# Two transformer layers on one core: blocks 1 and 2 by groups of four chunks, softmax attention of a sequence between the next one's groups, key projection folded into the query

## The chip, the cores and the metric

The program runs on one core of a Trainium2 chip. The metric is the device time of one execution in microseconds (us); smaller is better. Everything is computed in fp32 except one helper tile in bf16. The engines are PE (TensorE, matrix products, which write to PSUM banks), DVE (VectorE), ACT (ScalarE, activation functions), POOL (GpSimd) and SP, which issues the transfers. Each engine works through a queue of its own in order; semaphores make one wait for another.

## What is computed

The input is 8 sequences of 1024 rows of 256 numbers. Four blocks follow one another, each with a layer norm in front and an addition behind. Cut to what matters:

```python
# block 1: decoder layer with linear "flow" attention, 16 heads of 16, causal sums
q, k = sigmoid(heads(Wq, bq)), sigmoid(heads(Wk, bk)); v = heads(Wv, bv)
sink_in  = normal / einsum(q + EPS, cumsum(k) + EPS)          # normal = 1, 2, 3, ...
src_out  = normal / einsum(k + EPS, cumsum(q) + EPS)
cons_sink = einsum(q + EPS, cumsum(k * src_out) + EPS) / normal
cons_src  = clip(einsum(k + EPS, cumsum(q * sink_in) + EPS) / normal, -1, 1)
src_comp = exp(cons_src) / cumsum(exp(cons_src)) * normal
x = (q * sink_in / normal) @ cumsum(k^T (v * src_comp)) * sigmoid(cons_sink)
h = layernorm(inputs + x @ Wo + bo); out1 = layernorm(h + gelu(h @ W1 + b1) @ W2 + b2)
# block 2: feed-forward
relu(x @ w1 + b1) @ w2 + b2
# block 3: attention over the whole sequence, one head of 256
Q, K, V = split(t @ W_qkv.T + b_qkv); softmax(Q @ K.T / 16) @ V
# block 4: gated layer, inputs and weights rounded to FP4 by blocks of 16
fp4_linear(silu(fp4_linear(x, w_gate)) * fp4_linear(x, w_up), w_down)
```

The sums of block 1 run along the sequence, so a chunk of rows needs the sums over the chunks before it. Softmax attention needs the keys and values of all 1024 rows before its first row can be done.

## The kernel before

Rows are handled in chunks of 128 (the partitions), 8 chunks a sequence; four chunks are a group (`G`), two groups a sequence (`NG`). The weights stay in on-chip memory for the whole run. Sequences follow one another in a plain Python loop (L381), unrolled into one long program; a sequence goes stage by stage over all its 8 chunks:

- **Projection** (L386 to L415): layer norm, transposes on PE, one product for query and key (L397), one for the value (L401), additions on DVE, sigmoid on ACT. POOL prepares the residual `res`. The next sequence's input is then requested (L418).
- **Head sums** (L437 to L453), twice over the chunks: `head_sums` adds up a chunk's causal sums by a product with a triangular matrix (L354) and one with a matrix of ones for the chunks before (L356), whose sum POOL carries along in `summed` (L365); DVE does L429, L431 and L432 and the weighting L449.
- **Normalisers** (L456 to L490) by group: exponentials, their running sums, scaling of `v4`.
- **Attention of block 1** (L496 to L618) in four steps a chunk: `score` (transposes, products by head pairs L511, causal mask L519), `attend` (32 small records L544, the sums over earlier chunks L533 and L560), `project` (output product L586 and layer norm), `turn` (transpose into `hT`). `staggered` (L368) runs the steps of several chunks shifted against one another, the last step first, and after each step calls `fill`, which advances the first feed-forward (FFN1) of a group already complete.
- **FFN** (`ffn`, L195): eight hidden tiles of 128 x 512, each two matmuls and an activation; then, chunk by chunk, eight matmuls (L217) and the chunk's `finish`. FFN1 uses Gelu and closes block 1; block 2 (FFN2, Relu) follows for both groups (L623 to L643) after a layer norm of four chunks each.
- **Query, key, value** (L649 to L680) for the two groups: eight products of 512 columns for query and key (L653), and the values.
- **Softmax attention and block 4** (L688 to L784), again four staggered steps a chunk: `attention` (two score banks L695, maximum L702, Exp L710), `values` (transposes of the probabilities, L731, layer norm, FP4 rounding), `gate` (two halves of 352 columns, four banks, L752, Silu L759, product L760, FP4 rounding of 704 columns), `down` (transposes L769, product L773, output).

The FP4 rounding of the weights is a generator, `fp4_weights`, of 14 pieces, called from inside `ffn` after every second hidden tile of the first sequence (L212).

On-chip buffers come from pools with a fixed count: `t256` 8, `t512` 15, `t704` 5, `r256` 11, `r512` 10, `r1024` 7, six PSUM banks for products (`mm_bank`) and two for transposes. A tile can be written only when an earlier user of its buffer is done. The framework that builds the program orders each engine's queue itself from the instructions' dependencies and their place in the program, so a queue may differ from the order of the Python code.

Of the kernel before, what the change touches and what calls it, by code (L numbers as in the profile page):

```python
# [31 lines left out]
def block_stack_kernel(ctx: ExitStack, tc: tile.TileContext, a: dict, out: bass.AP):  # L32
# [8 lines left out]

    nc = tc.nc
# [17 lines left out]
    def t256(name):  # L60
        t = wk.tile([P, D], F32, tag="t256", name=name, bufs=8)
        return t

    def t512(name):
        t = wk.tile([P, 512], F32, tag="t512", name=name, bufs=15)
        return t

    def r256(name):
        t = big.tile([P, D], F32, tag="r256", name=name, bufs=11)
        return t  # L70

    def r512(name):
        t = big.tile([P, 512], F32, tag="r512", name=name, bufs=10)
        return t

    def r1024(name):
        t = big.tile([P, G, D], F32, tag="r1024", name=name, bufs=7)
        return t
# [43 lines left out]
    def load_x(s):  # L122
        tiles = []
        for g in range(NG):
            xg = r1024("xg")
            nc.sync.dma_start(
                out=xg,
                in_=x_dram[s, g * GT : (g + 1) * GT, :].rearrange("(c p) d -> p c d", p=P),
            )
            tiles.append(xg)  # L130
        return tiles

    x_next = load_x(0)
# [23 lines left out]
    wsm = load_tiles("L1_attn_W_qkv", 3 * D, 2)  # L157
    bsm = load_cols("L1_attn_b_qk", 4)
    bsv = load_row("L1_attn_b_v", D)
    wgT = const.tile([P, 2, INTER], F32, name="wgT")  # L160
# [33 lines left out]

    def ffn(inT, wa, ba, func, wb, finish):  # L195

        hidden = []
        for f in range(NF):
            bank = mm_bank()
            for k in range(2):  # L200
                nc.tensor.matmul(  # L201
                    bank,
                    lhsT=wa[:, k, f * P : (f + 1) * P],
                    rhs=inT[:, k, :],
                    start=k == 0,
                    stop=k == 1,
                )
            hf = t512("hidden")
            nc.scalar.activation(hf, bank, func, bias=ba[:, f : f + 1])
            hidden.append(hf)  # L210
            if f % 2:
                next(weight_pieces, None)  # L212
            yield
        for c in range(G):
            bank = mm_bank()
            for f in range(NF):
                nc.tensor.matmul(  # L217
                    bank[:, :D],
                    lhsT=hidden[f][:, c * P : (c + 1) * P],
                    rhs=wb[:, f, :],  # L220
                    start=f == 0,
                    stop=f == NF - 1,
                )
            finish(c, bank[:, :D])
            yield
# [7 lines left out]
    def fp4_exact(src, dst, rows, width, temp):  # L233
# [7 lines left out]
        amax = small([P, INTER // QB], "q_amax", 2)[:rows, :nb]  # L241
# [4 lines left out]
        s = small([P, INTER // QB], "q_s", 2)[:rows, :nb]  # L246
        r = small([P, INTER // QB], "q_r", 2)[:rows, :nb]
# [64 lines left out]
    def t704(name):  # L312
        t = wk.tile([P, INTER], F32, tag="t704", name=name, bufs=5)
        return t

    def fp4_weights():

        for name, dstT in (("L1_ffn_w_gate", wgT), ("L1_ffn_w_up", wuT)):
            for r0, rows in INTER_TILES:
                raw = t704("w_raw")  # L320
                nc.sync.dma_start(out=raw[:rows, :D], in_=a[name][r0 : r0 + rows, :])
                quant = t704("w_quant")
                fp4_exact(raw, quant, rows, D, t704)
                bank = pt.tile([P, 4, P], F32, tag="tr", name="tr")
                for k in range(2):
                    nc.tensor.transpose(
                        bank[:, k, :rows], quant[:rows, k * P : (k + 1) * P], ident[:rows, :rows]
                    )
                nc.scalar.copy(dstT[:, :, r0 : r0 + rows], bank[:, 0:2, :rows])
                yield  # L330
        for n in range(2):
            raw = t704("w_raw")
            nc.sync.dma_start(out=raw, in_=a["L1_ffn_w_down"][n * P : (n + 1) * P, :])
            quant = t704("w_quant")
            fp4_exact(raw, quant, P, INTER, t704)
            for k, (f0, rows) in enumerate(INTER_TILES):
                bank = pt.tile([P, 4, P], F32, tag="tr", name="tr")
                nc.tensor.transpose(bank[:rows, 0, :], quant[:, f0 : f0 + rows], ident)
                nc.scalar.copy(wdT[:rows, k, n * P : (n + 1) * P], bank[:rows, 0, :])
            yield  # L340
# [27 lines left out]
    def staggered(stages, n, between=None):  # L368


        for step in range(n + len(stages) - 1):
            for k in range(len(stages) - 1, -1, -1):
                if 0 <= step - k < n:
                    stages[k](step - k)
                    if between is not None:
                        between()
# [4 lines left out]
    for s in range(B):  # L381
        xs = x_next


        qk, v4, res = [], [], []
        for c in range(NCH):  # L386
            g, i = divmod(c, G)
            n0 = t256("n0")
            layernorm(n0, xs[g][:, i, :])
            n0T = t256("n0T").rearrange("p (k t) -> p k t", k=2)  # L390
            transposed(n0T, halves(n0), nc.scalar.copy)
            rc = r256("res0")
# [15 lines left out]
            qkc = r512("qk")  # L408
# [3 lines left out]
            if i == 0:  # L412
                vg = r1024("v4")
                v4.append(vg)
            nc.vector.tensor_tensor(v4[g][:, i, :], vbank[:, :D], bqkv[:, 2 * D :], ALU.add)  # L415

        if s + 1 < B:
            x_next = load_x(s + 1)  # L418


        groups = range(NG)
        s1 = [small([P, G, 2 * H], "s1", 2) for _ in groups]
        s2 = [small([P, G, 2 * H], "s2", 2) for _ in groups]
        r1 = [small([P, G, 2 * H], "r1", 2) for _ in groups]

        def head_sums(dst, c, cur, before):

            qke = t512("qke")
            nc.vector.tensor_scalar(qke, qk[c], ATT_EPS, None, ALU.add)  # L429
            bank = cumulated(cur, before)  # L430
            nc.vector.scalar_tensor_tensor(qke, bank, ATT_EPS, qke, ALU.add, ALU.mult)  # L431
            nc.vector.tensor_reduce(dst, heads(qke), AX.X, ALU.add)  # L432

        def over_heads(v, g, n):
            return v[:, g * G : (g + 1) * G].unsqueeze(2).to_broadcast([P, G, n])

        carry = None  # L437
        for c in range(NCH):
            head_sums(s1[c // G][:, c % G, :], c, qk[c], carry)
            carry = summed(carry, qk[c]) if c + 1 < NCH else None  # L440
        carry = None
        for g in groups:
            nc.vector.reciprocal(r1[g], s1[g])
            flow = small([P, G, 2 * H], "flow", 2)
            nc.vector.tensor_tensor(flow, r1[g], over_heads(pos, g, 2 * H), ALU.mult)
            for i in range(G):
                c = g * G + i
                w = t512("w")
                nc.vector.tensor_tensor(  # L449
                    heads(w), heads(qk[c]), per_head(flow[:, i, :], 2 * H), ALU.mult  # L450
                )
                head_sums(s2[g][:, i, :], c, w, carry)
# [374 lines left out]
```

## Time and profile before

| | |
|---|---|
| median of 3 runs | 4282.09 us (4281.36 to 4286.14) |
| profiled execution, its own time | 4281.81 us |
| its span, first to last instruction | 4280.1 us |
| mean granted TensorE clock | 0.868 |
| table loads on ACT (L710, L759, L410, L461, L209, one more) | 56 + 56 + 8 + 8 + 8 + 1, 1283 ns each |
| second sequence | 571 to 1101 us |
| first softmax attention's Exp | 371.5 us |

In the page, busy time is given by engine with its share of the span and its number of instructions. A chain of waits is followed back from the last instruction: what released it, or what ran before it on its engine. The granted clock is the share of full speed at which TensorE was let run. A busy TensorE is not TensorE at its best: matmuls are pipelined and their recorded ends are modelled, so the distance from start to start says more than the length of one.

### The profile page before, as it was taken

The page shows a single profiled execution, that of the slowest core. Times are in us where ns is not written, and L with a number is a line of the kernel's source. Part 1 is how long each engine was busy: PE and PEld are TensorE (multiplying, and loading weights), DVE is VectorE, ACT ScalarE, POOL GpSimd, SP SyncE. Part 2 cuts the span into 40 slices and gives each one's busy share as a digit, 9 for nine tenths or more (in the row PEclk, how much of TensorE's full clock was granted, in tenths as well). Part 3 has the DMA queues.
Part 4 walks back from the last instruction along what each step waited for, and adds up shares of the span by engine and source line. Part 5 has one row for each costly group of instructions (what it writes and reads, how often), then busy time and mean ns, then how long its engine had stood idle before and what let it go on. Part 6 is the DMA issues. An engine that isn't in the chain of part 4 may idle for free.

```text
span 4280.1 us, 38297 instructions
## 1 busy us (share of the span) xinstructions
PE 3559.5 (83%) x14180; PEld 2416.9 (56%) x14180; DVE 2096.5 (49%) x4817; ACT 926.7 (22%) x1774; POOL 717.3 (17%) x1297
## 2 busy tenths in 40 slices
PE   7878879888798877988779888898778987789877
PEld 5645557455574555755556555565556655566554
DVE  7675464245642456424564245642456324573244
ACT  1122311223112231122311123111221112211132
POOL 4220031200311003210031200312003120031100
PEclk8889897898888988899888988889888898888988
DMA  3000000000000000000000000000000000000000
GB/s 93 5 11 5 7 13 1 0 2 7 13 1 0 3 5 13 1 0 3 7 12 1 0 3 7 12 1 0 3 7 12 1 1 4 5 2 1 0 4 7
DMA packets 25738, 28.88 MB, mean 7 GB/s; under 512 B 2256, under 2 KB 24528, under 8 KB 25552
## 3 DMA queue, kind: packets, MB, share of 16 engines
q1 hardware_dynamic: 25552, 26.43, 2.0%
q8 instruction: 113, 1.85, 0.2%
q14 instruction: 73, 0.60, 0.0%
HBM read 18.03 MB, written 8.39 MB: 6 GB/s over the span
## 4 chain that ended last, share of the span: by engine, by line
PE 61%; DVE 25%; ACT 6%; POOL 4%; issue 4%; DMA 0%; ACTq 0%; DVEq 0%; POOLq 0%
PE mm L201 12%; PE mm L217 8%; PE mm L773 8%; PE mm L752 8%; PE mm L544 6%; PE tr L189 4%; PE mm L397 3%; PE mm L653 2%; PE mm L511 2%; POOL ln_rstd L173 2%; DVE x_amax L295 2%; DVE n L178 2%; DVE ln_st L167 2%; DVE qke L431 1%; DVE s L432 1%
## 5 line engine op out<-in xcount | busy, mean ns | idle before, releaser
L171 POOL TENSOR_SCALAR ln_ve<-ln_mv 128x1 f32<-128x1 f32 x384 | 107.7, 280 | 2718.7 <-DVE ln_mv L169 2703.0
L773 PE MATMUL mm<-wdT,hqT 128*128 128x256 f32 (+1 forms) x768 | 351.6, 615 | 174.7 <-ACT hqT L190 174.7
L773 PEld LDWEIGHTS mm<-wdT,hqT 128*128 128x128 f32 (+1 forms) x768 | 219.1, 313 | 279.7 <-ACT hqT L190 192.6
L544 PEld LDWEIGHTS mm<-v,sc 128*128 128x128 f32 x2048 | 279.2, 218 | 8.8 <-DVE sc L519 8.8
L544 PE MATMUL mm<-v,sc 128*128 128x16 f32 x2048 | 277.6, 279 | 3.0 <-DVE sc L519 3.0
L201 PE MATMUL mm<-hT,w_L_attn_W 128*128 128x512 f32 x512 | 271.1, 678 | 3.3 <-ACT hT L190 3.2
L201 PE MATMUL mm<-nT,w_L_ffn_w 128*128 128x512 f32 x512 | 252.7, 655 | 7.4 <-ACT nT L190 7.4
L189 PE MATMUL tr<-ident,n 128*128 128x128 f32 x512 | 122.9, 330 | 163.1 <-DVE n L178 111.2
L217 PE MATMUL mm<-w_L_attn_W,hidden 128*128 128x256 f32 x1024 | 251.0, 406 | 0.0
L731 PE MATMUL mm<-vt,probT 128*128 128x256 f32 x1024 | 242.9, 392 | 1.2 <-DVE rsum L727 0.8
L217 PE MATMUL mm<-w_L_ffn_w,hidden 128*128 128x256 f32 x1024 | 231.1, 379 | 0.0
L217 PEld LDWEIGHTS mm<-w_L_attn_W,hidden 128*128 128x128 f32 x1024 | 209.2, 206 | 38.5 <-issue 7.7
L695 PE MATMUL mm<-kT,qT 128*128 128x512 f32 x512 | 230.2, 592 | 0.0
L173 POOL TENSOR_TENSOR ln_rstd<-ln_ve,neghalf 128x1 f32<-128x1 f32 x384 | 218.8, 572 | 28.5
L731 PEld LDWEIGHTS mm<-vt,probT 128*128 128x128 f32 x1024 | 197.1, 198 | 29.4 <-DVE rsum L727 2.9
L217 PEld LDWEIGHTS mm<-w_L_ffn_w,hidden 128*128 128x128 f32 x1024 | 191.0, 190 | 30.5 <-issue 7.2
L637 DVE TENSOR_TENSOR res<-mm,res 128x256 f32<-128x256 f32 x64 | 27.1, 424 | 368.7 <-PE mm L217 368.7
L189 PEld LDWEIGHTS tr<-ident,n 128*128 128x128 f32 x512 | 63.4, 161 | 248.9 <-issue 192.3
L519 DVE TENSOR_TENSOR sc<-mm,triu 128x512 f32<-128x512 f32 x256 | 160.9, 684 | 87.7 <-PE mm L511 86.7
L760 DVE TENSOR_TENSOR hid<-hid,mm 128x352 f32<-128x352 f32 x128 | 66.7, 521 | 271.6 <-PE mm L752 265.2
L752 PE MATMUL mm<-wgT,xqT 128*128 128x352 f32 x512 | 185.8, 487 | 6.1 <-ACT xqT L190 3.7
L201 PEld LDWEIGHTS mm<-nT,w_L_ffn_w 128*128 128x128 f32 x512 | 106.5, 212 | 145.4 <-issue 131.6
(179 smaller groups left out, 6020.5 us busy)
## 6 DMA issues: line engine op xcount, KB each, us to landing
xg<-in_L_attn_inputs_dram SPq DMA_DIRECT2D x16, 512.0 KB, 4.8
out_dram<-y SPq DMA_DIRECT2D x64, 128.0 KB, 1.7
w_L_attn_W<-in_L_attn_W_dram SPq DMA_DIRECT2D x2, 1024.0 KB, 8.8
w_L_ffn_w<-in_L_ffn_w_dram SPq DMA_DIRECT2D x2, 1024.0 KB, 10.5
w_L_attn_W_qkv<-in_L_attn_W_qkv_dram SPq DMA_DIRECT2D x1, 768.0 KB, 8.5
w_raw<-in_L_ffn_w_down_dram SPq DMA_DIRECT2D x2, 352.0 KB, 2.8
w_raw<-in_L_ffn_w_gate_dram SPq DMA_DIRECT2D x5, 128.0 KB, 2.0
w_raw<-in_L_ffn_w_up_dram SPq DMA_DIRECT2D x5, 128.0 KB, 2.0
```

What stands on the lines that cost most here:

```text
L171: nc.gpsimd.tensor_scalar(ve, mv[:, 1:2], LN_EPS, 1.0, ALU.add, ALU.mult)
L173: nc.gpsimd.tensor_tensor(rstd, ve, neghalf, ALU.pow)
L189: nc.tensor.transpose(bank[:, i, :], src, ident)
L201: nc.tensor.matmul(bank, lhsT=wa[:, k, f * P : (f + 1) * P], rhs=inT[:, k, :], start=k == 0, stop=k == 1,)
L217: nc.tensor.matmul(bank[:, :D], lhsT=hidden[f][:, c * P : (c + 1) * P], rhs=wb[:, f, :], start=f == 0, stop=f == NF - 1,)
L397: nc.tensor.matmul(bank, lhsT=n0T[:, k, :], rhs=wqkv[:, k, : 2 * D], start=k == 0, stop=k == 1)
L519: nc.vector.tensor_tensor(sc, bank.rearrange("p (n t) -> p n t", n=4), triu.unsqueeze(1).to_broadcast([P, 4, P]), ALU.mult,)
L544: nc.tensor.matmul(bank[:, h * DH : (h + 1) * DH], lhsT=scores[r][:, 2 * k + e, :], rhs=v4[g][:, i, h * DH : (h + 1) * DH], start=kv is No ...
L695: nc.tensor.matmul(bank, lhsT=qT[e][g][:, i * P : (i + 1) * P], rhs=kT[e][kb], start=e == 0, stop=e == 1,)
L731: nc.tensor.matmul(bank[:, :D], lhsT=probT[j // G][:, j % G, :], rhs=vt[j // G][:, j % G, :], start=j == 0, stop=j == NCH - 1,)
L752: nc.tensor.matmul(bank, lhsT=xqT[:, k, :], rhs=wT[:, k, cols], start=k == 0, stop=k == 1,)
L773: nc.tensor.matmul(bank[:, :D], lhsT=hqT[k // 4][:rows, k % 4, :], rhs=wdT[:rows, k, :], start=k == 0, stop=k == len(INTER_TILES) - 1,)
```

## The change

Blocks 1 and 2 are now done a group at a time, from the input to the end of block 2, by a generator `group`; what the chunks before add (sums of query and key, of the weighted ones, of the exponentials, of key and value products) is carried from group to group in `past`. FFN1 is no longer advanced between the steps of block 1's attention. `ffn` keeps two PSUM banks in which the four chunks' results add up, each hidden tile being used as soon as it is there, and the four `finish` calls follow at the end; FFN1's `finish` takes in the layer norm and transposes for FFN2, FFN2's those for the values and the value product. All weight pieces (now 18, of at most 256 columns) are called after every hidden tile.

Softmax attention and block 4 became a generator too, `attention_and_fp4`. That of a sequence is advanced by one piece after every second piece of the next sequence's `sequence`, and the rest is done at once if any is left.

Keys are no longer projected. A product of the key and query weights is made once (`softmax_weights`), divided by 16; the query is projected with it chunk by chunk, and the scores are its products with the normed rows `n2T` themselves. The key bias adds the same number to a whole row of scores and falls out of the softmax.

Buffers: `t256` 9, `t512` 13, `t704` 3, and one pool for each kept kind: `xg` 2, `res` 12, `qk` 5, `v4` 2, `inT` 2, `n2T` 3, `vt` 3.

```diff
     def ffn(inT, wa, ba, func, wb, finish):
-        hidden = []
-        for f in range(NF):
...
-            if f % 2:
-                next(weight_pieces, None)
+        acc = [mm_bank(), mm_bank()]
+        before = None
+        for f in range(NF + 1):
+            hidden = None
+            if f < NF:
+                bank = mm_bank()
...
+                hidden = t512("hidden")
+                nc.scalar.activation(hidden, bank, func, bias=ba[:, f : f + 1])
+            if before is not None:
+                for c in range(G):
+                    h, half = divmod(c, 2)
+                    nc.tensor.matmul(
+                        acc[h][:, half * D : (half + 1) * D],
+                        lhsT=before[:, c * P : (c + 1) * P],
+                        rhs=wb[:, f - 1, :],
...
+            before = hidden
+            next(weight_pieces, None)
             yield
         for c in range(G):
...
+            h, half = divmod(c, 2)
+            finish(c, acc[h][:, half * D : (half + 1) * D])
             yield
```

```diff
+    def softmax_weights():
...
+                nc.tensor.matmul(
+                    bank[:, :D],
+                    lhsT=turned[0][:, f, e * P : (e + 1) * P],
+                    rhs=turned[1][:, f, :],
...
+            nc.scalar.mul(wqk[:, e, :], bank[:, :D], 1.0 / 16.0)
...
-    def staggered(stages, n, between=None):
+    def staggered(stages, n):
         for step in range(n + len(stages) - 1):
             for k in range(len(stages) - 1, -1, -1):
                 if 0 <= step - k < n:
                     stages[k](step - k)
-                    if between is not None:
-                        between()
+                    yield
```

```diff
+    def group(s, g, past, res, n2T, vt):
...
+        for i in range(G):
...
+            nc.vector.tensor_tensor(v4[:, i, :], vbank[:, :D], bqkv[:, 2 * D :], ALU.add)
+            yield
...
+        carry = past.get("qk")
+        for i in range(G):
+            head_sums(s1[:, i, :], qk[i], qk[i], carry)
+            carry = None if last and i == G - 1 else summed(carry, qk[i])
+            yield
...
+        yield from staggered([score, attend, project, turn], G)
...
+            layernorm_affine(xc, u, ln2g, xg[:, i, :])
+            n = t256("n")
+            layernorm(n, xc)
+            transposed(nT[:, :, i * P : (i + 1) * P], halves(n), nc.scalar.copy)
+            nc.gpsimd.tensor_tensor(xc, xc, fb2, ALU.add)
+        yield from ffn(hT, w1, b1, AF.Gelu, w2, finish)
...
+        yield from ffn(nT, fw1, fb1, AF.Relu, fw2, finish)
```

```diff
+    def attention_and_fp4(s, res, n2T, vt):
...
         def attention(c):
             g, i = divmod(c, G)
+            qT = two(t256("qT"))
+            bank = mm_bank()
+            for e in range(2):
                 for k in range(2):
                     nc.tensor.matmul(
+                        bank[:, e * P : (e + 1) * P],
+                        lhsT=wqk[:, k, e * P : (e + 1) * P],
+                        rhs=n2T[g][:, k, i * P : (i + 1) * P],
...
+            for e in range(2):
+                nc.scalar.activation(
+                    qT[:, e, :], bank[:, e * P : (e + 1) * P], AF.Identity, bias=bqk[:, e : e + 1]
+                )
...
+                        bank, lhsT=qT[:, e, :], rhs=n2T[kb][:, e, :], start=e == 0, stop=e == 1
...
-        staggered([attention, values, gate, down], NCH)
+        yield from staggered([attention, values, gate, down], NCH)
+
+    later = None
+    for s in range(B):
+        state = ([], [], [])
+        for piece, _ in enumerate(sequence(s, *state)):
+            if s == 0 and piece == 0:
+                softmax_weights()
+            if later is not None and piece % 2:
+                next(later, None)
+        for _ in later or ():
+            pass
+        for _ in weight_pieces:
+            pass
+        later = attention_and_fp4(s, *state)
+    for _ in later:
+        pass
```

## The prediction, made before the changed kernel was run

> **What bounds the kernel now.** I read the page's busy shares and chain of waits first, then the busy time by stage for one of the eight sequences, then the order of time inside the attention stage.
>
> ```profile
> PE 3559.5 (83%) x14180; PEld 2416.9 (56%) x14180; DVE 2096.5 (49%) x4817; ACT 926.7 (22%) x1774; POOL 717.3 (17%) x1297
> PE 61%; DVE 25%; ACT 6%; POOL 4%; issue 4%; DMA 0%; ACTq 0%; DVEq 0%; POOLq 0%
> ```
>
> TensorE carries most of the chain that ended last and VectorE a quarter. An average says no more, so here is the second sequence cut by stage: projections, head sums, attention of block 1 mixed with the first feed-forward (FFN1) of chunks 0 to 3, FFN1 of chunks 4 to 7, the second feed-forward (FFN2), query/key/value, softmax attention with the FP4 layer. The columns are window, length, busy time (and instructions) of PE, PEld, DVE, ACT and POOL, granted clock, DMA share, GB/s.
>
> ```profile
> 571.00:602.00 31.00, 26.71 (x85) 15.11 (x86) 16.17 (x33) 8.00 (x16) 17.96 (x27) 0.94 0.13 39
> 602.00:643.00 41.00, 32.25 (x149) 25.22 (x147) 39.44 (x75) 3.59 (x6) 15.61 (x21) 0.98 0.00 1
> 643.00:757.00 114.00, 105.62 (x610) 84.38 (x607) 55.10 (x124) 14.97 (x30) 21.95 (x39) 0.81 0.00 1
> 757.00:788.00 31.00, 29.60 (x98) 18.82 (x98) 6.88 (x18) 5.87 (x9) 3.73 (x7) 0.94 0.00 1
> 788.00:872.00 84.00, 67.85 (x224) 41.22 (x225) 19.57 (x56) 16.59 (x31) 17.97 (x40) 0.88 0.00 0
> 872.00:893.00 21.00, 20.93 (x67) 12.19 (x66) 7.21 (x16) 3.12 (x5) 0.74 (x2) 1.00 0.00 1
> 893.00:1101.00 208.00, 160.05 (x547) 103.78 (x545) 104.58 (x249) 61.76 (x120) 10.32 (x26) 0.84 0.02 6
> ```
>
> Only the head sums are VectorE's (39.4 of 41 us). The longest stage, 208 us, has no full engine: PE 77%, DVE 50%, and a granted clock of 0.84. Its order of time shows why; columns are start, length, engine, line, work, idle before and releaser.
>
> ```profile
> 562.71 1.12 PE L189 MATMUL tr<-ident,hid 128*128 128x128 f32 x4 [7.19 <-DVE hid L310]
> ...
> 565.78 4.27 PE L773 MATMUL mm<-wdT,hqT 128*128 128x256 f32 x10
> ...
> 882.31 7.03 PE L653 MATMUL mm<-n2T,w_L_attn_W_qkv 128*128 128x512 f32 x16
> ...
> 944.97 3.62 PE L731 MATMUL mm<-vt,probT 128*128 128x256 f32 x16
> ...
> 957.80 1.22 PE L773 MATMUL mm<-wdT,hqT 128*128 128x256 f32 x2 [4.08 <-ACT hqT L190]
> ```
>
> Undisturbed, 16 records of 256 columns take 3.62 us, 0.215 each once the last one's tail is left off. After the waits of 4.08 and 7.19 us ten such records take 4.27, 0.42 each: half the clock. So a wait is paid twice. (A matmul of fp32 is two records here.)
>
> A rule and this row: the Trainium skill, "TensorE: Matmul & The Clock Gate", Part 1, puts the clock at half after about 3.4 us of idling and back at full after about as much work. By it a wait of 2.97 us (which also stands in this stage) would cost nothing more; the row behind one such wait still shows 4.48 us for the ten.
>
> **PE work with nothing in its way.** By start-to-start distances at full clock: 512 columns 0.43 us (L653 above), 352 columns 0.295 (four in 1.18), 256 columns 0.215, a transpose 0.11 (four in 0.44), a 16-column record of L544 0.107 (16 in 1.71), a 32-row record of L511 0.068. Per group of four chunks:
> - projection 4 x (4 x 0.43 + 4 x 0.215 + 0.24) = 11.3
> - head sums and normalisers, 32 x 0.215 + 0.4 = 7.3
> - block 1's attention 4 x (32 x 0.107 + 16 x 0.068 + 8 transposes + 4 x 0.215 + 8 records of 128 at about 0.13) = 29.6
> - each FFN 32 x 0.43 + 64 x 0.215 = 27.5, with 1 us of transposes
> - value projection 16 x 0.215 = 3.4.
>
> That is 108 a group. Query and key add 32 x 0.43 = 13.8 a sequence, attention and FP4 8 x (8 x 0.43 + 16 x 0.215 + 16 x 0.295 + 12 x 0.215 + 2.0) = 130. A sequence holds 216 + 14 + 130 = 360 us of PE work and takes 530: 170 us are waits and half clock. This is what more independent work on PE can win.
>
> **The change, part by part.**
>
> *Key folded into query.* The 32 records of 512 columns (13.8 us) become 8 x 8 records of 128 columns, at 0.11 like transposes 7.0 us. DVE loses 4 x 0.748 = 3.0 us, ACT exchanges 4 x 0.687 for 16 x 0.27 (a 128-column copy, the hqT row) = +1.6. The new step from product through ACT stands ahead of each chunk's scores, some 1 us, under other pieces. Gain 3 to 7 us a sequence, in the PE figures below. The one-off product of the weights (8 transposes, some 32 records) is under 10 us; its two loads replace two thirds of the old 768 KB one.
>
> *FFN with two held banks.* The same matmuls in another order. What is new is at the end: all four chunks finish together, where finishes used to lie under the next chunk's 3.45 us of matmuls. FFN1's finish now has both layer norms, DVE 0.42+0.43+0.18+0.48+0.49 and 0.42+0.18+0.46 = 3.1 us a chunk, 13 to 14 with its POOL waits (ln_rstd 0.57); FFN2's is 2.3, so 9. The work isn't new, only bare where no other piece is there. Two of six matmul banks are held meanwhile.
>
> *By groups, without the old fill.* Block 1's attention of chunks 4 to 7 used to have FFN1 of chunks 0 to 3 between its steps; that is gone. A group alone, as a chain: projection 4 x 3.7 (the spacing of its transposes) = 15; sums 41/2 = 20.5; normalisers 6 (from the last sum to the first attention); attention steps 4 x 8.3 + 3.5 + 6 = 43; FFN1 27.5 + 14; FFN2 28.5 + 9. Sum 164.
>
> *Attention between.* A group has 4+4+4+1+16+13+13 = 55 pieces, every second calls one of 32 attention pieces (8 chunks x 4): 27 fall into the first group, 5 into the first nine pieces of the second. An attention chunk holds 17.1 us PE (with the query) and 13 DVE (104.6/8).
>
> First group, the larger of the two engines in each stage:
> - projection, 0.5 chunk: PE 11.3 + 8.6 = 20
> - sums and normalisers, 1.1 chunks: DVE 25 + 14.6 = 40
> - attention of block 1, 2 chunks: PE 29.6 + 34.2 = 64 (DVE 52)
> - FFN1, 1.6 chunks: PE 28.5 + 27.8 = 56
> - FFN2 with values, 1.6 chunks: 60.
>
> Sum 240, with 10% for waits in order (PE idles 17% now) 265. Second group: 164 + 5 for the attention pieces beyond the idle PE time of its sums, less 34 which neighbours cover: the queues are not in the program's order (layer-norm statistics of the next sequence stand at 541 us amid attention), so its projection goes under the first group's FFN finishes, and the next sequence's projection and first sums under its own. 135. So 400 a sequence.
>
> *Ends.* The first sequence has nothing to mix in: 2 x 164 - 15 + 10 of start. Its 18 weight pieces now all fall in its first two FFNs: the quantising rows sum to 127 us of DVE, of which some 56 fit (79 us of FFN less 23 of finishes), so +71: 394. The last attention stands alone: 208, +2.
>
> Sum: 394 + 7 x 400 + 210 = 3404, against 4281.8 of the profiled execution (span 4280.1 and 1.7 around it), which is within 0.3 us of the median. Predicted: **3400 us**.
>
> *Table loads.* ACT loads a table 137 times, 1.283 us each. Sigmoid and Gelu now stand between Exp and Silu pieces: FFN1 alone has 3 such breaks, some 5 to 8 more loads a sequence, 6 to 10 us of ACT. ACT is 22% busy, so I take it at nothing; were it all on the path, 70 us in all. The Trainium skill, "ScalarE: Activation LUTs", Table sets, says to batch calls by set, which speaks against this change, and gives 2.66 us a switch with its drain; by that the whole would be up to 150 us.
>
> **Rivals.** (a) *The second group stays bare and the first mixes only half*: A queue that waits in order holds up both streams. First group halfway between 240 and serial (164 + 6.75 x 26 = 340), 290; second uncovered, 169; table loads 10: 394 + 7 x 469 + 210 = 3890. For it: 170 us of waiting in a kernel that was already ordered to avoid it. Against: attention's waits are VectorE and ACT steps of one chunk, other chunks of work are ready.
>
> (b) *Slower, through matmul banks*: FFN holds two of six, a score step wants four, a gate four, so a piece can't start until the other stream gives banks back and the streams take turns. Serial: first group 340, second 164 + 1.25 x 26 = 197, loads 10: 547, and 394 + 7 x 547 + 210 = 4430. It decides from 525 a sequence on ((4281 - 604)/7). For it: all four gate banks wait for ACT's Silu and DVE's product (L759, L760). Against: such a reader takes only 0.46 to 0.69 us (L759, L710).
>
> (c) *Full cover*: the second group too is filled, 353 us of PE a sequence: 350 + 7 x 353 + 205 = 3030. Against: attention pieces are used up nine pieces into it, and block 1's chain starts from carried sums.
>
> (d) *The fold alone counts, mixing does nothing*, because the queues are reordered anyway: this gives 4282 - 8 x 5 = 4240. Against: at 562 us PE waited 7.19 with the next sequence's input statistics made.
>
> **Chances.** My case (3080 to 3850) 0.72, (a) and (d) up to no change 0.11, (c) 0.03, (b) 0.13, within 0.2% 0.01. About 0.2% is what a measurement of this kernel can tell from no change. So faster 0.86, same 0.01, slower 0.13; range 3080 to 3900, which leaves out some of (a), (c) and (b).
>
> **What would show it.** Right: granted clock above 0.93 and PE without a wait of over 4 us in the first group's stretch; that stretch 240 to 290 us, the second 120 to 170; 8 query records of 128 columns a chunk and no key rows; table loads 180 to 200. Wrong: waits on PE for banks' readers (DVE hid, ACT prob) growing in the FFNs; first and second group lasting alike. If the second group stays above 170, the cover I took for it failed.

## The result, and the profile after

The changed kernel takes 4385.11 us (median of 4 runs, 4381.08 to 4388.29) beside 4281.73 for the kernel before on the same chip (4 runs): 1.0239 times as long, 95% interval 1.0221 to 1.0256. It is slower by 2.4%; 3400 was predicted, and the range ended at 3900. The profiled execution has a span of 4384.6 us at a granted clock of 0.843 (before 0.868).

The two lines of the page that answer to those shown of before, busy time and the chain of waits by engine:

```profile
PE 3540.4 (81%) x14460; PEld 2494.9 (57%) x14460; DVE 2098.9 (48%) x4873; ACT 1026.2 (23%) x1945; POOL 733.9 (17%) x1293
PE 70%; DVE 17%; ACT 6%; POOL 4%; issue 3%; DMA 1%; SPq 0%; ACTq 0%; DVEq 0%; POOLq 0%
```

The busy shares hardly moved (PE 83 to 81%, DVE 49 to 48%); on the chain PE took over from DVE (61 to 70%, 25 to 17%). That doesn't say where the time went, so it is looked for by stage. Third sequence, columns as in the prediction (window, length, busy time of PE, PEld, DVE, ACT and POOL, granted clock, DMA share, GB/s). First group: projection, sums, block 1, FFN1, its finish, FFN2, its finish; then the same seven of the second group; last, the final sequence's attention.

```profile
1017.00:1041.00 24.00, 21.08 (x80) 13.23 (x79) 9.41 (x23) 9.29 (x17) 8.91 (x14) 1.00 0.00 1
1041.00:1084.00 43.00, 34.95 (x144) 25.25 (x142) 37.72 (x82) 12.53 (x25) 9.13 (x15) 0.95 0.00 1
1084.00:1167.00 83.00, 77.58 (x414) 60.45 (x414) 47.23 (x109) 18.01 (x39) 12.76 (x20) 0.84 0.01 4
1167.00:1224.00 57.00, 51.16 (x182) 33.92 (x181) 14.64 (x33) 22.00 (x37) 0.74 (x2) 0.91 0.01 3
1224.00:1255.00 31.00, 17.67 (x59) 12.44 (x58) 18.60 (x44) 5.35 (x10) 10.58 (x20) 0.72 0.07 21
1255.00:1301.00 46.00, 45.97 (x175) 30.38 (x174) 15.07 (x33) 14.03 (x25) 0.74 (x2) 1.00 0.01 3
1301.00:1324.00 23.00, 15.63 (x62) 10.54 (x62) 11.55 (x42) 7.34 (x17) 7.27 (x18) 0.93 0.02 7
1324.00:1357.00 33.00, 26.08 (x85) 16.14 (x84) 17.76 (x37) 9.50 (x17) 6.97 (x11) 0.84 0.00 1
1357.00:1395.00 38.00, 29.75 (x123) 22.36 (x122) 28.51 (x48) 7.52 (x15) 6.93 (x6) 0.91 0.02 7
1395.00:1452.00 57.00, 50.48 (x265) 42.45 (x266) 25.42 (x56) 4.73 (x12) 9.82 (x18) 0.58 0.00 1
1452.00:1481.00 29.00, 29.00 (x96) 18.50 (x95) 0.54 (x2) 6.46 (x9) 0.00 (x0) 0.94 0.00 0
1481.00:1501.00 20.00, 2.77 (x11) 1.20 (x9) 11.28 (x31) 1.49 (x4) 9.99 (x20) 0.62 0.09 26
1501.00:1531.00 30.00, 30.00 (x95) 19.09 (x96) 0.40 (x2) 5.50 (x8) 0.00 (x0) 0.91 0.00 1
1531.00:1541.00 10.00, 6.77 (x27) 4.77 (x27) 6.76 (x25) 1.74 (x5) 4.55 (x12) 0.83 0.00 1
...
4156.00:4384.00 228.00, 167.20 (x600) 110.75 (x598) 104.11 (x232) 66.03 (x132) 9.56 (x16) 0.87 0.02 5
```

Three things stand out. The finishes of FFN1 leave PE nearly empty: 2.77 us of 20 in the second group. Block 1 of the second group has PE busy for 50.48 of 57 us at a clock of 0.58. And the stages follow one another without overlap; the second group's first projection product comes at 1323.7, right behind the first group's last finish. Against the prediction:

| part | predicted | measured |
|---|---|---|
| first sequence | 394 | 495 |
| first group | 265 | 307 |
| second group | 135 | 217 |
| last attention | 210 | 229 |

A sequence takes 523 us against 529.6 before: seven times 7 won, 131 lost in the first sequence, 19 at the end, together +101 of the measured +103.

The waits on PE changed their kind, not their sum. From 1101 to 1630 us before, PE idled 85.5 us (22.1 for attention's `hqT`, 17.1 for its `hid`); from 1541 to 2065 after, 85.2 (4.7 for `hqT`, but 34.1 for the layer-normed `n`, most of it in the finishes).

The finish of FFN1 in the second group, in order of time, shows these (start, length, work, idle before and releaser), and the DVE instructions of one chunk below them why:

```profile
1485.43 0.41 PE L190 MATMUL tr<-ident,n 128*128 128x128 f32 x2 [4.18 <-DVE n L179]
1490.21 0.66 PE L190 MATMUL tr<-ident,n 128*128 128x128 f32 x2 [4.36 <-DVE n L179]
1494.98 0.66 PE L190 MATMUL tr<-ident,n 128*128 128x128 f32 x2 [4.11 <-DVE n L179]
1499.76 0.66 PE L190 MATMUL tr<-ident,n 128*128 128x128 f32 x2 [4.11 <-DVE n L179]
```

```profile
1485.21 0.41 DVE L652 TENSOR_TENSOR u<-mm,res 128x256 f32<-128x256 f32 x1
1485.65 0.43 DVE L168 BATCH_NORM_STATS2 ln_st<-u 128x6 f32<-128x256 f32 x1
1486.12 0.18 DVE L170 BATCH_NORM_AGGREGATE ln_mv<-ln_st 128x2 f32<-128x6 f32 x1
1486.34 0.48 DVE L183 SCALAR_TENSOR_TENSOR u<-u,ln_mv,b_L_attn_ln_g 128x256 f32<-128x256 f32 x1
1487.54 0.48 DVE L184 SCALAR_TENSOR_TENSOR res<-u,ln_rstd,xg 128x256 f32<-128x256 f32 x1 [0.72 <-POOL ln_rstd L174]
...
1489.65 0.41 DVE L179 TENSOR_SCALAR n<-res,ln_mv,ln_rstd 128x256 f32<-128x256 f32 x1 [0.95 <-POOL ln_rstd L174]
1489.98 0.42 DVE L652 TENSOR_TENSOR u<-mm,res 128x256 f32<-128x256 f32 x1
```

One chunk's chain, with two waits on POOL, is issued to its end before the next chunk's L652, 4.77 us after its own: four in series, although they don't depend on each other.

### The profile page after: what moved, and what is told of

Its sections match the earlier page's. It is cut to its first block, busy times and chain, and to the rows that moved or that the text cites. A ratio compares the mean times of both kernels' runs of the same rounds, so it can differ in the third digit from the quotient of the medians.

```text
span 4384.6 us, 38943 instructions
## 1 busy us (share of the span) xinstructions
PE 3540.4 (81%) x14460; PEld 2494.9 (57%) x14460; DVE 2098.9 (48%) x4873; ACT 1026.2 (23%) x1945; POOL 733.9 (17%) x1293
## 4 chain that ended last, share of the span: by engine, by line
PE 70%; DVE 17%; ACT 6%; POOL 4%; issue 3%; DMA 1%; SPq 0%; ACTq 0%; DVEq 0%; POOLq 0%
PE mm L209 11%; PE mm L222 10%; PE mm L762 7%; PE mm L593 7%; PE mm L783 6%; PE mm L741 6%; PE mm L709 4%; PE tr L190 4%; PE mm L464 2%; POOL ln_rstd L174 2%; PE mm L561 2%; PE mm L409 2%; PE mm L676 2%; DVE ln_st L168 2%; PE mm L632 2%
## 5 line engine op out<-in xcount | busy, mean ns | idle before, releaser
L593 PEld LDWEIGHTS mm<-v,sc 128*128 128x128 f32 x2048 | 317.0, 243 | 22.5 <-DVE v L539 17.9
L593 PE MATMUL mm<-v,sc 128*128 128x16 f32 x2048 | 313.8, 298 | 17.2 <-DVE v L539 17.2
L783 PE MATMUL mm<-wdT,hqT 128*128 128x256 f32 (+1 forms) x768 | 259.9, 483 | 56.2 <-ACT hqT L191 56.2
L741 PE MATMUL mm<-vt,probT 128*128 128x256 f32 x1024 | 271.6, 425 | 28.6 <-ACT probT L191 28.0
L709 PE MATMUL mm<-n2T,qT 128*128 128x512 f32 x512 | 239.2, 610 | 33.6 <-ACT qT L701 33.0
L209 PE MATMUL mm<-inT,w_L_ffn_w 128*128 128x512 f32 x512 | 262.8, 644 | 4.2 <-ACT inT L191 4.2
L209 PE MATMUL mm<-inT,w_L_attn_W 128*128 128x512 f32 x512 | 260.6, 637 | 4.3 <-ACT inT L191 4.2
L783 PEld LDWEIGHTS mm<-wdT,hqT 128*128 128x128 f32 (+1 forms) x768 | 169.4, 242 | 126.8 <-ACT hqT L191 67.3
L222 PEld LDWEIGHTS mm<-w_L_ffn_w,hidden 128*128 128x128 f32 x1024 | 191.7, 190 | 73.3 <-issue 50.2
L191 ACT COPY inT<-tr 128x256 f32<-128x256 f32 x128 | 47.8, 374 | 600.6 <-PE tr L190 600.6
L762 PE MATMUL mm<-wuT,xqT 128*128 128x352 f32 x512 | 174.6, 464 | 0.0
```

The costliest lines, as they stand in the source:

```text
L209: nc.tensor.matmul(bank, lhsT=wa[:, k, f * P : (f + 1) * P], rhs=inT[:, k, :], start=k == 0, stop=k == 1,)
L222: nc.tensor.matmul(acc[h][:, half * D : (half + 1) * D], lhsT=before[:, c * P : (c + 1) * P], rhs=wb[:, f - 1, :], start=f == 1 and half == 0,
L593: nc.tensor.matmul(bank[:, h * DH : (h + 1) * DH], lhsT=scores[r][:, 2 * k + e, :], rhs=v4[:, i, h * DH : (h + 1) * DH], start=kv is None, ...
L709: nc.tensor.matmul(bank, lhsT=qT[:, e, :], rhs=n2T[kb][:, e, :], start=e == 0, stop=e == 1)
L741: nc.tensor.matmul(bank[:, :D], lhsT=probT[j // G][:, j % G, :], rhs=vt[j // G][:, j % G, :], start=j == 0, stop=j == NCH - 1,)
L762: nc.tensor.matmul(bank, lhsT=xqT[:, k, :], rhs=wT[:, k, cols], start=k == 0, stop=k == 1,)
```

## The experiments

All give one time unless an interval is named. In these runs the kernel before took between 4279.5 and 4291.4 us, so some 10 us between single times tell nothing. e1 to e4 ran beside 4282.09 us of before, e5 to e8 beside 4291.4, e9 to e12 beside 4281.89, e13 and e14 beside 4286.99. The expectations name their theories by letters.

**e1**, the changed kernel without mixing:

```diff
-            if later is not None and piece % 2:
-                next(later, None)
...
+        for _ in attention_and_fp4(s, *state):
+            pass
```

> The changed kernel with the attention of a sequence run straight after it, nothing between the groups. Theory A (grouping costs, mixing gives most of it back): a bare group takes 180 us as in the first sequence of the changed kernel, a bare attention 228 as in its last; 495 + 7 x 360 + 8 x 225 = 4800, at least 4650. Theory B (the mixing itself is the loss, two streams hold each other up): no slower than the changed kernel's 4385, near 4280.

Measured 4891.31. Windows of its third sequence: first group, second group, attention.

```profile
1325.00:1507.00 182.00, 145.00 (x591) 104.11 (x592) 70.36 (x159) 26.65 (x49) 39.36 (x69) 0.79 0.01 3
1507.00:1691.00 184.00, 148.68 (x609) 106.33 (x608) 71.29 (x159) 26.81 (x49) 37.71 (x65) 0.80 0.01 4
1691.00:1919.00 228.00, 168.11 (x603) 111.35 (x604) 105.88 (x242) 66.77 (x135) 13.85 (x26) 0.87 0.02 5
```

Two bare groups take 366 us, value products included; before, blocks 1 and 2 took 301 (571 to 872) and the value products some 7, so grouping costs about 58 a sequence. Attention behind the new query costs another 20 (228 against 208), and the 14 of the query and key products are gone: 594 us a sequence against 530. In the changed kernel attention adds 125 to the first group (307 - 182) and 33 to the second (217 - 184), 158 in place of 228: mixing works and is worth 70 a sequence, 506 us in all. It about pays for the rest.

**e2**, before with the new `ffn`; **e4**, the changed kernel with the old one (the first diff; e2 is its reverse, in before); **e3**, before with the key fold (the second diff):

```diff
-        acc = [mm_bank(), mm_bank()]
...
+            hf = t512("hidden")
+            nc.scalar.activation(hf, bank, func, bias=ba[:, f : f + 1])
+            hidden.append(hf)
```

```diff
-                        lhsT=qT[e][g][:, i * P : (i + 1) * P],
-                        rhs=kT[e][kb],
+                        lhsT=qT[:, e, :],
+                        rhs=n2T[kb][:, e, :],
```

> The kernel before with only the feed-forward with two held banks and its finishes at the end. Theory A: the finishes are bare, serial by chunk: some 8 us more for each of the four feed-forwards of a sequence, 30 a sequence, about 4520. Theory C (the order of the feed-forward is free, freed buffers gain a little): 4260 to 4300.

> The kernel before with only the key projection folded into the query, the query made chunk by chunk. As predicted: 3 to 7 us a sequence gained, 4226 to 4258. Theory D (the added step from product through ACT to the scores stretches each attention chunk by some 2 us, as the last attention of the changed kernel suggests: 228 us against 208): 20 lost and 14 gained a sequence, about 4330.

> The changed kernel with the feed-forward of before (eight hidden tiles kept, product and finish chunk by chunk), mixing kept. Theory A: finishes go under the next chunk's matmuls again, second group 11 + 7 us, first group some 30 less: 45 to 50 a sequence, about 4000 to 4050. Theory E (eight hidden tiles of 13 buffers hold up the attention between): 4350 to 4500.

Measured: e2 4298.37 (+16, little beyond the scatter), e3 4371.99 (+90), e4 4507.98 (+123 to the changed kernel). The new `ffn` is not what made the kernel slow; the old one is worse there: in the first group of the third sequence FFN1 with its finishes lasts 88 us as in the changed kernel, but FFN2 88 instead of 68 (from first product to the next stage's first). Eight of 13 `t512` are held there while attention needs the same buffers; that these are the reason was only argued. The fold, for which a gain of 3 to 7 us a sequence was predicted, costs 90. PE in e3's attention, in order of time:

```profile
957.47 1.05 PE L724 MATMUL mm<-n2T,wqk 128*128 128x128 f32 x8
961.49 0.52 PE L194 MATMUL tr<-ident,hid 128*128 128x128 f32 x3 [2.96 <-DVE hid L318]
961.84 3.60 PE L740 MATMUL mm<-n2T,qT 128*128 128x512 f32 x8
...
969.24 0.70 PE L818 MATMUL mm<-wdT,hqT 128*128 128x256 f32 x2 [3.58 <-ACT hqT L195]
```

The query's product is done at 958.5, but its scores, 3.60 us of work that used to fill one of the waits, now stand behind a transpose that waits 2.96 us for DVE.

**e5** and **e6**: the query of a chunk made one chunk earlier, in e3 and in the changed kernel.

```diff
+        def attention(c):
+            if c == 0:
+                query(0)
+            qT = qTs.pop(c)
+            if c + 1 < NCH:
+                query(c + 1)
```

> The kernel before with the fold, but a chunk's query made one chunk ahead (with the scores of the chunk before). The fold alone took 4372. Theory D (the scores, which used to lie under the wait for the FP4 chain, came to stand behind it because their query wasn't there): back to 4230 to 4300. Theory F (the small records, their weight loads and two more activations a chunk are the cost): 4350 or more.

> The changed kernel with each chunk's query made one chunk ahead. If the fold costs there what it cost in the kernel before: 4385 - 90 = 4295. If the mixing covers the query's wait and only the bare last attention gains: 4350 to 4375.

Measured: e5 4208.22, 164 below e3 and 83 below its own before; e6 4352.99, 32 below the changed kernel. The wait on the query was the fold's cost, and with it out of the way the fold is a gain. In the changed kernel other pieces already covered much of it.

**e7**, the finishes issued step by step over the four chunks instead of chunk by chunk:

```diff
+            for i, y in enumerate(ys):
+                us.append(t256("u"))
+                nc.vector.tensor_tensor(us[i], y, res[g * G + i], ALU.add)
+                stats.append(ln_stats(us[i]))
...
+            for i in range(G):
+                xc = res[g * G + i]
+                nc.vector.scalar_tensor_tensor(
+                    xc, us[i], stats[i][1], xg[:, i, :], ALU.mult, ALU.add
+                )
+                stats[i] = ln_stats(xc)
```

> The changed kernel with the four chunks' finishes issued step by step over the chunks instead of chunk by chunk. Theory A (a finish is a serial chain of 4.8 us a chunk with VectorE waiting for GpSimd): second group 20 to 13 and 10 to 8 us, first group 31 to about 22: 15 to 20 a sequence, 4225 to 4265. Theory G (finish is bound by something else, or attention pieces fill it): 4360 to 4400.

Measured 4178.39, 207 below the changed kernel, more than expected. The same stretch of PE as above:

```profile
1427.67 0.66 PE L190 MATMUL tr<-ident,n 128*128 128x128 f32 x2 [7.30 <-DVE ln_mv L170]
1428.53 0.66 PE L190 MATMUL tr<-ident,n 128*128 128x128 f32 x2 [0.19 <-DVE n L668]
1429.83 0.66 PE L190 MATMUL tr<-ident,n 128*128 128x128 f32 x2 [0.64 <-DVE n L668]
1431.42 0.66 PE L190 MATMUL tr<-ident,n 128*128 128x128 f32 x2 [0.93 <-DVE n L668]
```

9.1 us of waiting in place of 16.8. The transposes come 1.3 us apart, not 4.77, and PE's idle time in a sequence falls from 85.2 to 67.1.

**e8**, the attention pieces put at chosen places, 16 in each group, four of them at FFN1's finishes and none beside the FFNs' matmuls; **e9**, the weight pieces after every second hidden tile:

```diff
-            if later is not None and piece % 2:
+            if later is not None and piece % 55 in PIECES:
```

```diff
-            next(weight_pieces, None)
+            if f % 2:
+                next(weight_pieces, None)
```

> The changed kernel with 16 attention pieces in each group, at projection, sums, attention of block 1 and first finish, none in the feed-forwards' matmuls. Theory A (mixing pays where TensorE waits, and the second group waits bare): about 40 a sequence less, 4100, at least below 4250. Theory H (each piece gains the same wherever it stands): 4350 to 4420.

> The changed kernel with the weight pieces called after every second hidden tile, as before, so that they reach over the four feed-forwards of the first sequence. The changed kernel's first sequence takes 495 us to its end, its second group 180 and its first, with all weight pieces, 315. If the pieces' VectorE work between the finishes is what makes the difference: first sequence 40 to 80 us shorter, 4305 to 4345. If it only moves: 4375 to 4395.

Measured: e8 4471.01, 86 longer, a miss. The first finish of its second sequence lasted 48 us: attention's steps and the serial finishes now stand in one another's way on DVE. There the last chunk's finish starts at 701.88 us, behind an addition of attention's output (L791) that waited 5.02 us for PE. e9 4339.48, 46 shorter, as expected.

**e10**, e7 with e6's and e9's edits; **e11**, the pieces of e10 moved to the FFNs; **e12**, one piece after every third, 16 in each group:

```diff
+    PIECES = (1, 4, 7, 10, 13, 16, 19, 22, 25, 28, 31, 34, 37, 40, 43, 46)
...
+            if later is not None and piece % 55 in PIECES:
```

> Staged finishes, query one chunk ahead and spread weight pieces together, mixing as changed. If the three are separate terms (207, 32 and some 60 us): 4085. If they share the same waits: 4130 to 4180.

> As the run before, with the attention pieces at the hidden tiles of the feed-forwards (16 in the first group, 10 in the second) and 6 at the first group's projection and sums. Theory H (a piece's own waits on VectorE and ScalarE are covered only where TensorE has dense work of its own, so pieces belong beside the feed-forwards' matmuls): 3980 to 4060, below the run before. Theory A (pieces belong where TensorE waits): above it, 4130 or more.

> As the run before last, with one attention piece after every third piece in both groups. If the bare second group was the loss: 4000 to 4050. If each placing costs the same: as the run before last, within 30.

Measured: e10 4080.28 (0.9523 of before, 0.9509 to 0.9537), near the sum of its terms (207 + 32 + 46 off 4385 is 4100). e11 4133.75 (0.9652, 0.9636 to 0.9668), worse than e10. e12 4018.52 (0.9381, 0.9367 to 0.9395). So an even spread does help here; that serial finishes alone spoiled e8 is not shown, since its pieces stood at other places too. Stretches of one sequence's length of e10, e11 and e12, and between them block 1 of e11's second group, where no piece was left:

```profile
1210.00:1698.00 488.00, 423.56 (x1800) 298.85 (x1800) 240.13 (x560) 126.44 (x236) 90.07 (x158) 0.89 0.02 5
```

```profile
1239.00:1288.00 49.00, 43.89 (x261) 37.24 (x262) 24.99 (x55) 3.59 (x9) 8.95 (x17) 0.65 0.00 1
1202.00:1700.00 498.00, 434.27 (x1800) 309.42 (x1800) 244.05 (x559) 126.52 (x236) 88.11 (x158) 0.86 0.02 5
```

```profile
1142.00:1623.00 481.00, 418.54 (x1800) 295.00 (x1799) 239.54 (x559) 123.27 (x234) 90.65 (x158) 0.89 0.02 5
```

PE idles nearly alike in the three, 63.9, 63.1 and 61.4 us. e11 differs in the clock. That led to the last question: e12 still takes 481 us where 400 were predicted, and in block 1 the clock is low although PE hardly waits. From the changed kernel, three slices of 1 us, in a stretch (1400.35 to 1431.07) in which no row of PE has a wait, and three runs of the same 16 records of 16 columns:

```profile
1416.00:1417.00 1.00, 1.00 (x12) 1.00 (x11) 0.48 (x1) 0.00 (x0) 0.40 (x2) 1.00 0.00 0
1417.00:1418.00 1.00, 1.00 (x10) 1.00 (x9) 0.00 (x0) 0.00 (x0) 0.52 (x1) 0.84 0.06 16
1418.00:1419.00 1.00, 1.00 (x6) 0.99 (x5) 0.42 (x1) 0.00 (x0) 0.00 (x0) 0.50 0.00 0
```

```profile
1416.18 2.07 PE L593 MATMUL mm<-v,sc 128*128 128x16 f32 x16
...
1424.89 1.86 PE L593 MATMUL mm<-v,sc 128*128 128x16 f32 x16
...
1436.50 3.43 PE L593 MATMUL mm<-v,sc 128*128 128x16 f32 x16
```

The clock falls from full to half within the first run, with PE busy all the time. Between the other two PE waited 0.25 and 0.16 us, and yet the last one takes 3.43 us against 1.86.

**e13** and **e14** change e12's narrow records. e13 gives each head's product 128 columns, the heads of a half adding up in one place, so that block 1's output is another one; e14 has one such product for the eight heads of a half and leaves the other seven out.

```diff
-                        bank[:, h * DH : (h + 1) * DH],
+                        bank[:, k * P : (k + 1) * P],
...
-                        rhs=v4[:, i, h * DH : (h + 1) * DH],
+                        rhs=v4[:, i, k * P : (k + 1) * P],
```

In e14 also:

```diff
-                for n in range(H // 2):
+                for n in range(1):
```

> The e12 kernel; in block 1's attention each head's product has 128 columns (the half it belongs to) instead of its own 16, same number of records; the heads of a half add up in one place, so block 1's output is another one. e12: 4018.5 us, 481 a sequence, of which 150 us are block 1's attention steps at a granted clock of 0.82, with PE 90% busy. Theory W (the half clock comes from PE's waits alone): the clock of this stretch stays at 0.80 to 0.84, and time is e12's within 30 us, or up to 60 longer as 128 columns take 0.11 to 0.13 a record against 0.107. Theory C (narrow records themselves let the clock fall, without a wait): the stretch's clock rises above 0.93, 10 to 20 us a sequence come back, 3860 to 3960 us in all.

> The e12 kernel; in block 1's attention one product of 128 columns stands for the eight products of 16 columns of a half: 28 records fewer a chunk, 7 of 8 heads' products left out. At 0.107 us a record at full clock that is 3.0 us a chunk, 24 a sequence, 190 in all if all of it is on the path. Theory W: time falls by 100 to 190 us, clock of block 1's stretch unchanged or lower, since waits for VectorE come closer together (3830 to 3920). Theory C: the records left out took the clock with them; the stretch's clock rises above 0.93 and time falls by 230 to 320 us (3700 to 3790).

Measured: e13 3910.42, 108 below e12 with eight times the columns; e14 3844.26. Block 1's attention with its pieces in e12, e13 and e14:

```profile
1200.00:1275.00 75.00, 67.62 (x372) 52.08 (x372) 44.08 (x102) 12.40 (x30) 12.49 (x22) 0.82 0.01 3
```

```profile
1171.00:1241.00 70.00, 61.89 (x373) 47.68 (x374) 45.20 (x102) 12.91 (x30) 12.83 (x22) 0.91 0.01 3
```

```profile
1149.00:1212.00 63.00, 50.20 (x256) 35.63 (x256) 42.63 (x102) 12.09 (x28) 12.31 (x22) 0.85 0.01 3
```

e13 decides for theory C, though its clock stayed a little under the 0.93 named: PE idles 65.0 us a sequence, no less than in e12 (61.4), so no wait was taken away, only the clock rose. By slices of 1 us e12's clock, once full, falls again at or just behind the runs of 16 columns (from 1219, 1243 and 1260 us on), and once behind a wait of 1.98 us (1274); e13's stays at 1.00 from 1185 to 1241. What is left of half clock there is the first 13 us, behind waits of 2.90 and 3.06 us. e14 is no clean test: without the records PE waits more (73.3 us a sequence), its clock rises only to 0.85, and its time lies in W's range.

**e15** makes e13's records give the heads' own sums, and **e16** does so with 64 columns:

```diff
+            nc.gpsimd.tensor_copy(
+                spread.rearrange("p k (n x) -> p k n x", x=P + DH)[:, :, :, :DH],
+                v4[:, i, :].rearrange("p (k n d) -> p k n d", k=2, d=DH),
+            )
...
-                        rhs=v4[:, i, h * DH : (h + 1) * DH],
+                        rhs=spread[:, k, n * P : (n + 1) * P],
```

> The e12 kernel with e13's wide records made to give the right sums: POOL lays each chunk's values into a buffer that is zero elsewhere, so that a record of 128 columns adds one head's 16 and zeros, and the eight heads of a half add up in one place. Room for it: v4 has 1 buffer, qk 4, t512 11. Theory C: e13's gain holds, 3910 plus the cost of the new copy; a POOL row of 256 elements is off PE's path if POOL (18% busy) makes it before the products, so 3900 to 3960. If the fewer buffers or the copy stand on the path, 8 chunks x 8 x up to 1 us: up to 3975. Theory W, which e13 speaks against: 4018 or above.

> The same with records of 64 columns (four heads add up in one place) and t512 left at 13. If a record's width is what holds the clock, and holds it in proportion, the gain lies between none at 16 columns (4018) and all at 128 (e15), and its clock in block 1's stretch between 0.82 and 0.91; if 64 columns are enough, it equals e15 within 15 us.

Measured beside 4285.89: e15 3906.20 (0.9115 of before, 0.9101 to 0.9128), the fastest that does the whole work; e16 3916.45 (0.9140, 0.9124 to 0.9155). 64 columns bring nearly all of it. The groups of these records by line (form and count, busy time and mean ns, idle before), first the narrow ones of the changed kernel, then e15's wide ones and POOL's new copy:

```profile
L593 PE MATMUL mm<-v,sc 128*128 128x16 f32 x2048 | 313.8, 298 | 17.2 <-DVE v L539 17.2
```

```profile
L597 PE MATMUL mm<-spread,sc 128*128 128x128 f32 x2048 | 252.2, 277 | 2.4 <-POOL spread L548 2.4
...
L548 POOL COPY spread<-v 128x256 f32<-128x256 f32 x64 | 26.8, 420 | 149.1 <-PE mm L597 90.8 <-DVE v L540 58.3
```

**e17**, the kernel before with e5's query and e16's records:

```diff
-                        rhs=v4[g][:, i, h * DH : (h + 1) * DH],
+                        rhs=spread[:, q, n % 4 * 64 : n % 4 * 64 + 64],
```

> The kernel before with e5's query one chunk ahead (4208 beside 4291) and e16's records of 64 columns. Its block 1 stretch is 95% busy PE at a clock of 0.78 to 0.81, as low as in the changed kernel. Theory C: the same gain as in e16 (some 100 us), so 4090 to 4130, which leaves 170 to 220 us between it and e16 as what groups and mixing bring by themselves once finishes, query and weights are put right. Theory W: 4190 to 4230, as the waits are untouched.

Measured 4139.75 beside 4282.39 (0.9666, 0.9650 to 0.9682), 68 below e5 (59 if each is set against its own before), a smaller gain than C expected and a larger one than W. Block 1's attention in the third sequence, before and in e17:

```profile
1169.00:1256.00 87.00, 82.63 (x508) 64.67 (x507) 43.65 (x96) 13.27 (x26) 16.26 (x30) 0.78 0.00 1
```

```profile
1132.00:1211.00 79.00, 73.86 (x513) 58.90 (x514) 45.31 (x100) 13.53 (x27) 19.85 (x41) 0.91 0.00 1
```

The loss of clock was there before the change. With the query ahead and the wider records on both sides, e16 is 223 us faster than e17: that is what groups, mixing and the new `ffn` bring once their finishes, weights and pieces are put right.

## Why the prediction was wrong, point by point

- **The second group, "less 34 which neighbours cover"**: the step that failed most clearly. None of PE's work was covered: each group's first product comes right behind the last one of the group before. The step "164 + 5" was short as well: a bare group takes 184 (e1), of it 54 for block 1 where 43 were taken, at a clock of 0.59, and 50 for FFN1 with its finishes where 41.5 were taken; and the few attention pieces left cost 33, not 5. 217 in place of 135 is 82 us seven times, 574 of the 985 us that the prediction was off. The prediction itself said that above 170 the cover failed.
- **Finishes, "13 to 14" and "9", "bare where no other piece is there"**: mis-sized, and bare with pieces too. They took 20 and 10 in the second group and 31 and 23 in the first. 3.1 us of DVE a chunk had been added up, with a microsecond or two of POOL for all four; the rows show two waits on POOL in every chunk (0.72 and 0.95) and 4.77 us a chunk in series. In the first group attention's own DVE steps come on top. With the finishes issued by steps the kernel takes 207 us less (e7).
- **First group 240, "with 10% for waits in order"**: 307. Projection, sums and FFN1's tiles came nearly as computed (24, 43 and 57 against 20, 40 and 56) and FFN2 with values 69 against 60. Outside of the sum were FFN1's finish, 31, and 19 us of block 1 (83 against 64), whose clock was 0.84.
- **"So a wait is paid twice", and a clock above 0.93 once the waits go**: half true. The rows after the waits show it (ten records in 4.27 us behind 7.19, in 3.97 behind the 4.08 that is shown), as do the first 13 us of e13's stretch. The 4.48 us behind a wait of 2.97 say less than was made of them: a wait of 0.97 and two transposes stand just ahead of it. And the half clock in block 1 needs no wait. The stage with 105.62 of 114 us busy at 0.81 stood in the prediction's own table and speaks against the reading given. e13 and e15 put this at some 110 us in e12 (in the changed kernel itself it wasn't measured), e17 at 59 to 68 in the one before. The Trainium skill, "TensorE: Matmul & The Clock Gate", Part 1, has the clock follow an activity window and fall after some 3.4 us without work. Here it fell from 1.00 to 0.50 within 2 us, 17 us into a stretch without a wait, so what counts as activity is more than being busy.
- **Key fold, "gain 3 to 7 us a sequence" with the step "under other pieces"**: wrong in place. Issued directly ahead of its scores it costs 90 us alone (e3); a chunk ahead the fold gains 83 (e5). In the changed kernel the order cost 32.
- **First sequence 394**: 495. Bare groups took 182 to 184 rather than 164, and e1's bare groups follow one another without the overlap for which 15 had been taken off. That leaves 129 us for the start and the weight pieces, where 10 and 71 had been taken; spread over four FFNs the pieces cost 46 less (e9).
- **Rival (b)**, slower by turns through the banks: its turning point of 525 us a sequence was nearly the measured 523, but the loss beyond it came from the first sequence, and the mechanism seen is order in DVE's and PE's queues. That banks were ever waited for was not shown, and a score step takes three of them (one for the query, two for the scores), not four.
- **Right**: the waits on `hqT` fell from 22.1 to 4.7 us a sequence, mixing wins time (506 us, e1), and table loads rose from 137 to 196 (180 to 200 predicted) whose cost no run took apart.

Not settled: e15 still takes 467 us a sequence against the predicted 400. PE idles 64.4 us of it, in waits such as 8.6 and 9.5 us ahead of transposes of `n`, and the clock is 0.93. Which order of pieces would fill these waits wasn't tried beyond e8, e11 and e12. Why narrow records let the clock fall isn't shown either, only that they do.

## What to carry to other kernels

Before counting a stage as covered by its neighbours, look in the trace whether instructions of the next stage ever stand in its waits; where several chunks end together, issue their finishing steps across the chunks, not chunk by chunk. A value for the matrix engine should be made a piece of work ahead of its use, since the waiting matmul also holds up what is queued behind it. Where the granted clock is low although TensorE is busy, look at how narrow its records are as well as for waits.

## What the runs showed of the hardware that had not been expected

TensorE's granted clock can fall to half under products of 16 columns issued without a gap: in the changed kernel from 1.00 at 1416 us to 0.50 at 1418, busy 1.00 of every 1.00 us. With 128 columns and the same count of records the clock in block 1's stretch is 0.91 (e13) instead of 0.82 (e12), and eight times the columns take 108 us less in all. At full clock a wide record costs hardly more: a run of 16 takes 1.78 us to the next record's start in e13 and 1.71 in e12, 0.111 and 0.107 a record. 64 columns do nearly as well (10 us behind, e16).
